# Attention at the layer border: 0.4 chunk for each q, and second-block steps between the last q

## The chip, the cores and the metric

The kernel runs on one core of a Trainium2 chip. TensorE (PE), VectorE (DVE), ScalarE (ACT), GpSimd (POOL) and SyncE (SP) are five engines, each with its own queue of instructions; they wait for one another by semaphores. DMA queues, fed mostly by SP and POOL here, move data between HBM and SBUF. The metric is the device time of one execution in microseconds (us); the time of a kernel is the median of its runs.

## The reference

Two layers of a graph transformer on 2708 tokens with 512 features, 8 heads, float32 throughout. The adjacency matrix is sparse (a token has a few neighbours, at most 22 here), so attention needs only the listed neighbours of each token. One layer, cut to what is computed:

```python
q = (h @ Wq.T + bq).reshape(n, N_HEADS, D_K)      # k and v likewise
scores = jnp.einsum('nhd,mhd->hnm', q, k) / jnp.sqrt(D_K)
scores = jnp.where(mask[None, :, :] == 0, -1e9, scores)   # mask = adj + eye
ctx = jnp.einsum('hnm,mhd->nhd', softmax(scores), v).reshape(n, D_MODEL)
h1 = layer_norm(h + ctx @ Wo.T + bo, ln1_g, ln1_b)
ff = relu(h1 @ W1.T + b1) @ W2.T + b2             # D_FF = 2048
h2 = layer_norm(h1 + ff, ln2_g, ln2_b)            # the next layer's h
```

Layer 0's h2 is layer 1's h.

## The kernel before

Tokens are sorted by their number of neighbours and cut into 22 tiles of 128 (the last has 20). Two tiles make a block, eleven blocks make a layer; the first block of a layer is tiles 21 (20 rows, 2 chunks of neighbours) and 20 (128 rows, 3 chunks), the second is tiles 19 (3 chunks) and 18 (4 chunks).

**Attention** is a generator, `attend`. A chunk is up to two neighbours of every token of a tile. For each chunk POOL gathers the rows of k and v by an indirect DMA (line 982) into one of five kv buffers; DVE multiplies k with q (L1019) and reduces per head to scores (L1025); a step later ACT takes the exponential (L1038) and, for the chunk's second neighbour, scales v head by head (L1045, eight small copies), DVE scales the first neighbour's v (L1051) and adds to the sum (L1058). After a tile's last chunk come its sums (L1066 to L1081) and the division on ACT (L1089), which leaves `cx`. Each `next` of the generator emits one such step and yields its cost: 1.0 for a chunk of two neighbours, 0.5 for one, 0.2 for an empty step. After the first block there are three empty steps, so its eight steps cost 1.0 + 0.5 + 1.0 + 1.0 + 0.5 + 3 x 0.2 = 4.6.

**Pacing.** `advance(more)` adds to a credit (at most 1.5) and emits steps while the credit is above zero and fewer than two finished tiles lie in `got`. `through(k)` emits steps until block k's tiles are in `got`, whatever the credit.

**The border** is the stretch between layer 0's last feed-forward and layer 1's first. There the projections of q of layer 1 run on PE: sixteen tiles, each four matmuls of 512 columns (L569), an evacuation on DVE (L1226) into one of three row buffers, and a write of q to HBM by SP (L1236). The first eight read transposed tokens that were loaded ahead (`pool`), the last eight are streamed: `queries` loads a tile's tokens by SP (L1213), yields, and projects it at the next call. Between the projections the loop advances the first block's attention. Then `through(0)` makes sure that the block is complete; `attended` transposes `cx` (L1128, evacuated as `cT` by ACT, L1133), loads the block's residual `xb` (L979, SP), multiplies by Wo (L569, `o`), adds and normalises (L1254, then L1112 to L1122, with a power on POOL, L1118). Behind that the last of the streamed steps run: two projections of q and the last write. Then `turned` transposes h (L1128) into `hT` (L1133, ACT), and the feed-forward (L1296, L1304, L1284) begins, with the second block's attention between its steps. A tile's q is read back by SP (L979) when its attention begins.

**Order.** The orders of PE, ACT and SP are those in which the program emits instructions. In the border DVE's is by hand as well, for what is emitted there; elsewhere a scheduler places DVE's and POOL's instructions, and it can place later DVE work of attention between those of the border.

The border in the code begins at line 1485 with:

```python
            with tc.manual_schedule(engines={mybir.EngineType.DVE}):
                for _ in range(2):
                    now.query(*pool.pop(0))
                next(ahead)
                next(streamed)
                while pool:
                    advance(0.5)
                    now.query(*pool.pop(0))
                for i in range(2 * AHEAD - 10):
                    advance(0.5)
                    next(streamed)
                through(0)
```

Of the kernel before, what the change touches and what calls it, by code (L numbers as in the profile page):

```python
# [471 lines left out]
def by_edges(ctx: ExitStack, tc: tile.TileContext, x, xT, adj, layers, out, good):  # L472
# [57 lines left out]
    def matrix(w, name, tag, by=None):  # L530
        src = chunked(w[name])
        t = wts.tile([P, src.shape[1], src.shape[2]], F32, tag=tag, name=tag)
        if by:
            by.dma_start(out=t, in_=src)
            return t
        k = max(1, src.shape[1] // 4)
        for c in range(0, src.shape[1], k):
            nc.sync.dma_start(out=t[:, c : c + k, :], in_=src[:, c : c + k, :])
        return t
# [32 lines left out]
    def finish(steps):  # L572
        for _ in steps:
            pass
# [416 lines left out]
    def asked(n, g):  # L991

        r = size(g)
        if g in own:
            return own.pop(g)
        if n == 0 and not all_made:
            return None
        q = at.tile([P, DM], F32, tag="q", name="q", bufs=QB)
        fetch(n, q, q_d[n], g)
        return q  # L1000
# [375 lines left out]
    def attend(n, got):  # L1376

        peak = small.tile([P, NT], F32, tag="peak", name="peak", bufs=1)
        nc.vector.memset(peak, 0.0)
        loaded = loads(n)  # L1380
        steps = []
        for g in order:
            cuts = chunks_of(g)
            steps += [(g, s0, c, i, i + 1 == len(cuts)) for i, (_, s0, c) in enumerate(cuts)]
            if g == order[1]:
                steps += [None] * 3
        steps += [None] * 3
        kv = next(loaded)
        yield 0.0
        q = asked(n, order[0])  # L1390
        done = [None] * 3
        for k, step in enumerate(steps):
            if step:
                g, s0, c, i, last = step
                if i == 0:
                    while q is None:
                        q = asked(n, g)
                        if q is None:
                            yield None
                    t, q = Tile(g, q), None  # L1400
                if k > 0:
                    kv = next(loaded)
                t.weights(kv, s0, c)
                if i > 0 and q is None and g != order[-1]:
                    q = asked(n, order[order.index(g) + 1])
                done.append((t, kv, s0, c, last))
            else:
                done.append(None)
            t3, t2, t1 = done[-4:-1]
            if t1:  # L1410
                t1[0].weigh(*t1[1:4])
            if t2 and t2[-1]:
                t2[0].sums(peak)
            if t3 and t3[-1]:
                got[t3[0].g] = t3[0].divided()
            yield c / SLOTS if step else 0.2
        nc.vector.tensor_reduce(flags[:, 4 + n : 5 + n], peak, AX.X, ALU.max)
        nc.vector.tensor_scalar(
            flags[:, 4 + n : 5 + n], flags[:, 4 + n : 5 + n], SAFE, None, ALU.is_le
        )  # L1420
# [3 lines left out]
    def advance(more):  # L1424

        nonlocal credit
        credit = min(credit + more, 1.5)
        while credit > 0 and len(got) < CXB - 1:
            cost = next(ahead, None)
            if cost is None:  # L1430
                break
            credit -= cost

    def through(k):

        while blocks[k][-1] not in got:
            next(ahead)
# [40 lines left out]
    for n in range(NL):  # L1478
        last = n == NL - 1
        nxt = None if last else Layer(n + 1, layers[n + 1])  # L1480
        if n > 0:
            streamed = now.queries(order[8 : 2 * AHEAD])
            got = {}
            ahead = attend(n, got)
# [3 lines that stand above are left out]
                next(ahead)  # L1488
                next(streamed)
                while pool:  # L1490
                    advance(0.5)
                    now.query(*pool.pop(0))
                for i in range(2 * AHEAD - 10):
                    advance(0.5)
                    next(streamed)
                through(0)
                early[n] = now.attended(blocks[0], got)
                next(early[n])
                for _ in blocks[0]:
                    next(early[n])  # L1500
                finish(streamed)
            now.load_w2(NFC // 2 - 1)
        *_, hs = early[n]
        hT = now.turned(blocks[0], hs)
        turning = projecting = None
        in_order = ExitStack()
        if n == 0:
            in_order.enter_context(tc.manual_schedule(engines={mybir.EngineType.Pool}))
        for k, block in enumerate(blocks):
            more = k + 1 < NB  # L1510
            asking = iter(())
            if n > 0 and k + AHEAD < NB:
                asking = now.queries(blocks[k + AHEAD])
            for f, zs in enumerate(now.feed_forward(block, hs, hT)):
                if f == NFC:
                    break
                if f in (5, 6, 7, 8) and behind:
                    next(behind)
                if more and f == 10 + (k + n == 0):
                    through(k + 1)  # L1520
                    projecting = now.attended(blocks[k + 1], got)
                    next(projecting)
                if more and f == 11 + (k + n == 0):
                    for hs_next in projecting:
                        advance(0.5 if k else 0.0)
                advance(PACE[n] if k else 1.1 if f < 11 else 0.4)
                if f in (0, 3, 7, 9):
                    next(asking, None)
                if more and f == NFC - 1:
                    finish(asking)  # L1530
                    hT = now.turned(blocks[k + 1], hs_next)
                if k == 0 and len(now.w1) < NFC // 2 and f % 2 == 0:
                    now.load_w1(len(now.w1), nc.scalar)
                    now.load_w2(len(now.w2), nc.scalar)
                if n > 0 and (k, f) == (0, 2):
                    now.load_second(1, temp)
                if not last:
                    if (k, f) == (0, 10):
                        now.load_next()
                        now.kv = [matrix(nxt.w, "Wk", "wk", nc.scalar)]  # L1540
                    if (k, f) == (0, 13):
                        now.kv.append(matrix(nxt.w, "Wv", "wv", nc.scalar))
                    if (k, f) == (3, 2):
                        now.wq = matrix(nxt.w, "Wq", "wq")
                    if f == 1 and k in (1, 3):
                        i, name, scale = (1, "bk", 1.0) if k == 1 else (0, "bq", DK**-0.5)
                        turning = turned_row(now.cols[i], name, scale)
                        rows_of = now if k == 1 else nxt
                        setattr(rows_of, name, next(turning))
                    if f == 3 and k in (1, 3):  # L1550
                        finish(turning)
                if not last and not more:
                    if f % 2:
                        nxt.load_w1(f // 2)
                        if f > 2:
                            nxt.load_w2(f // 2 - 1)
                    if f == 6:
                        nxt.load_first()
                        nxt.load_second(0, temp)
                    if f == 7:  # L1560
                        finish(ahead)
                        pool += nxt.preloaded(order[:8], temp)
            in_order.close()
            if not last:
                behind = now.keys_values(block, zs)
            if more:
                hs = hs_next
        finish(ahead)
        if last:
            checked()  # L1570
        else:
            nxt.wq = now.wq
            for _ in range(2):
                nxt.query(*pool.pop(0))
            nxt.kept()
            for g in order[:2]:
                own[g] = asked(n + 1, g)
            finish(behind)
            behind = None
            now = nxt  # L1580
# [63 lines left out]
```

## Time and profile before

| what | us |
|---|---|
| median of 3 runs | 1968.01 |
| lowest and highest run | 1963.77, 1973.71 |
| the profiled execution | 1964.63 |
| its span, first to last instruction | 1962.9 |
| PE busy in it | 1901.0 |
| DVE, ACT, POOL busy | 1300.8, 933.8, 796.8 |
| first q of layer 1 on PE to the first feed-forward matmul of layer 1 | 1138.33 to 1228.88 |

Times in the profile are microseconds from the span's start. A busy engine is one with an instruction in flight. A timeline row has start, duration, engine, line of the kernel, operation, tiles and shapes, number of instructions merged, and in brackets the idle time of the engine before it with what ended it. A PE matmul in float32 leaves two records, so x8 are four matmuls. A table of stretches gives busy times by engine, then the TensorE clock that was granted (1.00 is full) and the share of the DMA engines' time in use.

### The profile page before, as it was taken

The page shows a single profiled execution, that of the slowest core. Times are in us where ns is not written, and L with a number is a line of the kernel's source. Part 1 is how long each engine was busy: PE and PEld are TensorE (multiplying, and loading weights), DVE is VectorE, ACT ScalarE, POOL GpSimd, SP SyncE. Part 2 cuts the span into 40 slices and gives each one's busy share as a digit, 9 for nine tenths or more (in the row PEclk, how much of TensorE's full clock was granted, in tenths as well). Part 3 has the DMA queues.
Part 4 walks back from the last instruction along what each step waited for, and adds up shares of the span by engine and source line. Part 5 has one row for each costly group of instructions (what it writes and reads, how often), then busy time and mean ns, then how long its engine had stood idle before and what let it go on. Part 6 is the DMA issues. An engine that isn't in the chain of part 4 may idle for free. (4 is left out here: it accounts for less than half of the span.)

```text
span 1962.9 us, 20872 instructions
## 1 busy us (share of the span) xinstructions
PE 1901.0 (97%) x6162; PEld 1100.6 (56%) x6162; DVE 1300.8 (66%) x2142; ACT 933.8 (48%) x3219; POOL 796.8 (41%) x710
## 2 busy tenths in 40 slices
PE   8999988999999999999999998999999999999997
PEld 4444444565565655566556643556666566666664
DVE  5884587685867869659442036888688988877421
ACT  4660254564555655547332112756456765755410
POOL 3114635453555535425310022555347655644210
PEclk9999999999999999999999999999999999999998
DMA  9998766455655556546310646856455766554000
GB/s 327 352 311 307 258 211 235 161 166 189 202 161 199 188 186 227 161 150 204 130 43 27 230 162 215 298 174 217 153 177 198 247 214 209 186 190 154 34 11 13
DMA packets 131486, 366.92 MB, mean 187 GB/s; under 512 B 16668, under 2 KB 36988, under 8 KB 128654
## 3 DMA queue, kind: packets, MB, share of 16 engines
q0 software_dynamic: 69120, 246.35, 37.9%
q1 hardware_dynamic: 53332, 99.66, 14.9%
q10 hardware_dynamic: 8910, 19.48, 2.6%
q8 instruction: 50, 0.82, 0.2%
q14 instruction: 74, 0.61, 0.1%
HBM read 314.62 MB, written 50.83 MB: 186 GB/s over the span
## 5 line engine op out<-in xcount | busy, mean ns | idle before, releaser
L982 POOL DMA_INDIRECT kv<-kv_d,idx x420 | 546.1, 1300 | 475.9 <-DVE acc L1058 319.1
L1284 PE MATMUL a<-w,ft 128*128 128x512 f32 (+1 forms) x1408 | 669.9, 601 | 10.8 <-ACT ft L1304 9.5
L1296 PE MATMUL pf<-hT,w 128*128 128x256 f32 (+1 forms) x2816 | 636.3, 373 | 13.2 <-ACT ft L1304 8.8
L1296 PEld LDWEIGHTS pf<-hT,w 128*128 128x128 f32 x2816 | 521.1, 191 | 192.2 <-issue 107.3
L1284 PEld LDWEIGHTS a<-w,ft 128*128 128x128 f32 (+1 forms) x1408 | 256.5, 187 | 239.0 <-issue 201.4
L1304 ACT ACTIVATE ft<-pf,b 128x256 f32<-128x256 f32 (+1 forms) x352 | 158.5, 459 | 424.8 <-PE pf L1296 424.5
L1019 DVE TENSOR_TENSOR kv<-kv,q 128x1024 f32<-128x1024 f32 (+3 forms) x222 | 256.5, 1158 | 156.3 <-DMA kv<-kv_d,idx 103.7
L1045 ACT ACTIVATE kv<-kv,p 128x64 f32<-128x64 f32 x1232 | 311.0, 335 | 5.0
L1025 DVE TENSOR_REDUCE sc<-kv 128x16 f32<-128x1024 f32 (+3 forms) x222 | 255.2, 1154 | 1.4
L1058 DVE TENSOR_TENSOR acc<-acc,kv 128x1024 f32<-128x1024 f32 (+2 forms) x178 | 204.0, 1146 | 26.7 <-ACT kv L1045 25.9
L1118 POOL TENSOR_TENSOR rd<-va,mhalf 128x1 f32<-128x1 f32 (+1 forms) x88 | 85.4, 971 | 267.6 <-DVE va L1116 266.2
L1038 ACT ACTIVATE p<-sc,minus 128x8 f32<-128x8 f32 (+1 forms) x420 | 103.4, 295 | 161.1 <-DVE sc L1025 154.6
L569 PE MATMUL o<-wo,cT 128*128 128x512 f32 (+1 forms) x352 | 157.8, 601 | 3.7 <-DVE qs L1226 3.3
L1051 DVE TENSOR_TENSOR kv<-kv,p 128x512 f32<-128x512 f32 (+1 forms) x178 | 121.6, 684 | 52.8 <-ACT p L1038 52.7
L569 PEld LDWEIGHTS o<-wo,cT 128*128 128x128 f32 (+1 forms) x352 | 65.5, 187 | 92.2 <-issue 80.9
L1089 ACT ACTIVATE cx<-acc,su 128x64 f32<-128x64 f32 (+1 forms) x352 | 88.4, 333 | 42.6 <-DVE su L1081 33.9
L1316 DVE TENSOR_TENSOR h<-a,h 128x512 f32<-128x512 f32 (+1 forms) x44 | 29.7, 677 | 106.8 <-PE a L1284 106.7
L1122 DVE SCALAR_TENSOR_TENSOR h<-h,rd,ln_b 128x512 f32<-128x512 f32 (+1 forms) x88 | 65.9, 749 | 50.9 <-POOL rd L1118 50.9
L663 ACT ACTIVATE code<-aj 128x2708 bf16<-128x2708 int32 (+1 forms) x22 | 73.2, 3329 | 49.1 <-POOL aj L659 45.4
L1355 POOL DMA_INDIRECT kv_d<-kvs,ident_i x22 | 23.7, 1077 | 179.0 <-ACT kvs L1349 110.9
L666 DVE MAX8 tops<-code 128x8 f32<-128x247 f32 (+2 forms) x242 | 83.1, 400 | 19.3 <-ACT code L663 19.3
L1045 ACT ACTIVATE acc<-kv,p 128x64 f32<-128x64 f32 (+1 forms) x352 | 88.8, 334 | 1.4
(133 smaller groups left out, 1514.2 us busy)
## 6 DMA issues: line engine op xcount, KB each, us to landing
aj<-in_adj SPq DMA_DIRECT2D x21, 1354.0 KB, 8.0
kv_d<-kvs ACTq DMA_DIRECT2D x21, 512.0 KB, 5.6
w<-in_W SPq DMA_DIRECT2D x20, 512.0 KB, 4.8
xg<-in_xT SPq DMA_DIRECT2D x19, 512.0 KB, 8.8
kv<-kv_d,idx POOLq DMA_INDIRECT x420, 5.6
w<-in_W ACTq DMA_DIRECT2D x12, 512.0 KB, 8.9
q_d<-qs SPq DMA_DIRECT2D x22, 256.0 KB, 4.2
zT_d<-zT SPq DMA_DIRECT2D x22, 256.0 KB, 5.3
```

Of the source, the lines that this page charges most:

```text
L569: nc.tensor.matmul(o[:r], xs(c), wm[:, c, :], start=(c == 0), stop=(c == NC - 1))
L982: nc.gpsimd.indirect_dma_start(out=to, out_offset=None, in_=table[:, :], in_offset=bass.IndirectOffsetOnAxis(ap=s, axis=0), bounds_check=N ...
L1019: nc.vector.tensor_tensor(kv[:r, :c, :DM], kv[:r, :c, :DM], self.q[:r].unsqueeze(1).to_broadcast([r, c, DM]), ALU.mult,)
L1025: nc.vector.tensor_reduce(self.sc[:r, s0 : s0 + c, :], kv[:r, :c, :DM].rearrange("p s (h d) -> p s h d", d=DK), AX.X, ALU.add,)
L1038: nc.scalar.activation(p[:r, s, :], self.sc[:r, s, :], AF.Exp, bias=minus[:r, g, s : s + 1])
L1045: nc.scalar.activation(to[:, i, hd], kv[:r, i, DM + h * DK : DM + (h + 1) * DK], AF.Copy, scale=p[:r, s0 + i, h : h + 1],)
L1051: nc.vector.tensor_tensor(to[:, 0, :].rearrange("p (h d) -> p h d", d=DK), kv[:r, 0, DM:].rearrange("p (h d) -> p h d", d=DK), p[:r, s0, : ...
L1058: nc.vector.tensor_tensor(self.acc[:r, :c, :], self.acc[:r, :c, :], kv[:r, :c, DM:], ALU.add)
L1089: nc.scalar.activation(cx[:r, hd], self.acc[:r, 0, hd], AF.Copy, scale=self.su[:r, h : h + 1])
L1284: nc.tensor.matmul(a[:r], fts[f][:, c0 : c0 + r], self.w2[f // 2][:, f % 2, :], start=(f == 0), stop=(f == NFC - 1),)
L1296: nc.tensor.matmul(pf[:, :w], self.w1[f // 2][:, c, f % 2 * P : f % 2 * P + P], hT[:, c, :w], start=(c == 0), stop=(c == NC - 1),)
L1304: nc.scalar.activation(ft[:, :w], pf[:, :w], AF.Relu, bias=self.b1[:, f : f + 1])
```

## The change

Both loops of projections advance attention by 0.4 in place of 0.5 for each q. The last streamed steps, which ran straight through, now have an advance of 0.6 behind each of them; there are three such steps: a projection, a projection, and the last write.

```diff
@@ -1488,17 +1488,18 @@
                 next(ahead)
                 next(streamed)
                 while pool:
-                    advance(0.5)
+                    advance(0.4)
                     now.query(*pool.pop(0))
                 for i in range(2 * AHEAD - 10):
-                    advance(0.5)
+                    advance(0.4)
                     next(streamed)
                 through(0)
                 early[n] = now.attended(blocks[0], got)
                 next(early[n])
                 for _ in blocks[0]:
                     next(early[n])
-                finish(streamed)
+                for _ in streamed:
+                    advance(0.6)
             now.load_w2(NFC // 2 - 1)
         *_, hs = early[n]
         hT = now.turned(blocks[0], hs)
```

The advances behind the streamed steps emit steps of the second block, at a place where DVE's order is by hand.

## The prediction, made before the changed kernel ran

> **What bounds the kernel now.** I read the page's busy shares first, then a table of stretches across the border between the layers, then the timelines of TensorE (PE), VectorE (DVE) and ScalarE (ACT) there, and last the DMA issues of SyncE (SP).
>
> ```profile
> PE 1901.0 (97%) x6162; PEld 1100.6 (56%) x6162; DVE 1300.8 (66%) x2142; ACT 933.8 (48%) x3219; POOL 796.8 (41%) x710
> ```
>
> ```profile
> 1190.00:1200.00 10.00, 9.53 (x23) 3.98 (x22) 10.00 (x13) 1.47 (x6) 3.36 (x3) 1.00 0.68 212
> 1200.00:1205.00 5.00, 3.79 (x10) 1.53 (x9) 3.40 (x9) 2.02 (x8) 1.93 (x2) 1.00 0.91 304
> 1205.00:1210.00 5.00, 1.79 (x10) 0.77 (x9) 0.69 (x1) 0.78 (x4) 0.00 (x0) 0.87 0.86 315
> 1210.00:1217.00 7.00, 6.48 (x9) 1.26 (x10) 0.59 (x1) 0.59 (x3) 0.00 (x0) 0.60 0.31 89
> ```
>
> PE is busy for 97% of the span: a change wins only where PE idles or has a low clock. A row of the table is stretch and length, busy time of PE, weight loads, DVE, ACT and POOL, then granted clock, DMA share, GB/s. From 1205 to 1217 PE first idles and then works at clock 0.60. PE's timeline (start, duration, idle before it and its releaser) gives the reasons:
>
> ```profile
> 1180.91 7.03 PE L569 MATMUL q<-wq,zT 128*128 128x512 f32 x16
> 1189.67 3.70 PE L569 MATMUL q<-wq,zT 128*128 128x512 f32 x8 [1.74 <-DVE qs L1226]
> 1193.84 7.10 PE L569 MATMUL q<-wq,zT 128*128 128x512 f32 x16 [0.47 <-DMA zT<-zT_d]
> 1202.15 3.70 PE L569 MATMUL q<-wq,zT 128*128 128x512 f32 x8 [1.21 <-DVE qs L1226]
> ...
> 1210.07 6.30 PE L569 MATMUL o<-wo,cT 128*20 128x512 f32 x8 [3.27 <-DVE qs L1226]
> ...
> 1220.37 7.03 PE L569 MATMUL q<-wq,zT 128*128 128x512 f32 x16
> 1227.33 1.01 PE L1128 MATMUL tp<-ident,h 20*128 20x20 f32 x8
> 1228.88 4.31 PE L1296 MATMUL pf<-hT,w 128*128 128x148 f32 x32 [0.54 <-ACT hT L1133]
> ```
>
> Four stalls, 6.69 us, stand before the first o; from 1228.88, the start of the first feed-forward (FF), PE is busy without a gap until 1400. So 1228.88 is my yardstick: a shift there is carried to the end. DVE and ACT show whom PE waits for:
>
> ```profile
> 1187.74 1.23 DVE L1019 TENSOR_TENSOR kv<-kv,q 128x1024 f32<-128x1024 f32 x1 [3.09 <-DMA q<-q_d]
> 1188.99 1.22 DVE L1226 SCALAR_TENSOR_TENSOR qs<-q,bq 128x512 f32<-128x512 f32 x2
> ...
> 1209.23 0.69 DVE L1226 SCALAR_TENSOR_TENSOR qs<-q,bq 128x512 f32<-128x512 f32 x1 [5.83 <-DMA q_d<-qs]
> 1216.41 0.68 DVE L1254 TENSOR_TENSOR h<-o,xb 20x512 f32<-20x512 f32 x1 [6.49 <-PE o L569]
> ```
>
> ```profile
> 1216.41 1.14 ACT L1133 ACTIVATE cT<-tp,bv 128x128 f32<-128x128 f32 x4 [9.38 <-PE o L569]
> 1227.79 1.82 ACT L1133 ACTIVATE hT<-tp,b 128x20 f32<-128x20 f32 x8 [10.23 <-PE tp L1128]
> ```
>
> The kv line at 1187.74 is already the second block's (tile 19): DVE stalls there 3.09 us for that tile's q, with a finished q evacuation (L1226) queued behind it. The last evacuation waits 5.83 us, because its row buffer is still being written out. ACT is idle for 10.23 us before hT.
>
> ```profile
> DMA to landing us min/median/max: 3.2/4.4/7.5
> ```
>
> That is the 14 writes q_d<-qs from 1160 to 1230.
>
> [...]after 3.27 us idle one o took 6.30 us, where others of its shape take 3.43 (half of the x16 pitch), so 2.87 us lost. [...]
>
> **The change part by part.** The durations are of one profiled execution: span 1962.9, run 1964.63, which is 3.4 below the median 1968.01. I re-timed the border from the changed kernel's instruction order, built and not run, with each instruction at the duration of its row and each DMA at a landing time from this trace. Done so for the order of before, with 5.2 us for a write and 5.0 for a load, FF comes out at 1222.3, 6.6 early; the low clock (2.87), the slow q load (1.9) and the slow last write (1.8) are these 6.6. So those three are priced on their own below.
>
> *Loop at 0.4.* Ten advances give 4.0 instead of 5.0 of credit, but the first block's eight steps cost 4.6, and through(0) makes up the rest, so no work of the first block is removed. What changes is DVE's order: tile 19's three L1019/L1025 pairs (6 x 1.2 = 7.2 us) no longer stand between the q evacuations, and the 3.09 stall goes with them. The evacuation of 1188.99 can come at about 1184.7, the next when a q_d write issued at 1180.3 lands (4.4 later, 1184.7). PE's q then run on without a stall: two from 1180.91 to 1187.8, four more at 3.43 to 1201.5, 1.0 for the transposes, o at 1202.5 instead of 1210.07: 7.6 us earlier. It also comes warm (2.87). o for both tiles ends at 1202.5 + 6.9 + 0.6 (the cT wait, as now 0.46) = 1210.0 instead of 1220.37. **Gain here 10.4 us.** What is late next: not PE.
>
> *Advances behind the last three streamed steps.* They execute two steps of tile 19 before the FF: both weights, the first weigh, and by the order the second weigh too (on ACT before hT). Work is moved here from the first FF, where it was covered by PE. Now the path goes through DVE and ACT:
>
> - The order puts tile 18's first two L1019 into the norm of h: the first directly behind the 20-row L1254, with BNStats queued behind. It needs tile 18's q. On SP that load stands behind two xb loads and the last qs write. The 128-row xb load waits for a write issued at about 1199.0 to land (4.4 to 4.7: 1203.7), then two issues of 0.45: the q load goes out at 1204.6. To land takes 4.5 (median of q<-q_d) to 6.9 (1180.84 to 1187.74 in this border). I take 5.4: 1210.0. DVE, free at 1206.8, stalls 3.2 us.
> - From there both norms: before, L1254 to the next L1226 took 1216.41 to 1224.16 = 7.75. Without the first L1254 (0.69) and the 0.5 wait for o, plus two L1019 (2.3) of which 0.6 fills norm gaps: 8.3. L1226 at 1218.3.
> - Then 0.6 + 1.13 + 1.2 + 1.13 + 1.13 (a reduce of tile 18 that also got in) + 1.2 = 6.4: the second score at 1224.7.
> - ACT's two exps and eight copies of that chunk (0.48 + 2.02, less overlap: 2.4) stand in front of hT: hT starts at 1227.1. FF began 1.09 after hT before, so now at **1228.2: 0.7 earlier** than 1228.88. Of the gain of 10.4, 9.7 is eaten.
> - PE is done with its q at 1216.9 and has only transposes until 1228.2; it stalls about 9 us in front of FF, so FF starts at the low clock: +2.8 as in the measured case[...].
>
> Sum: -0.7 + 2.8 = **+2.1 us**. Tile 19's third weigh and ft are in time: ft is needed four pf (at least 4.4 us) after FF's start. POOL's four gathers for tile 18 wait for the first block's adds (L1058), which come earlier, so they go out some 3 to 6 us before 1195.68; rd (L1118), which both norms wait for, stands behind them in POOL's queue as before and is not held up. What is queued behind the new wait on DVE is BNStats, both norms and the last two q evacuations; PE's transposes of h, then hT and FF, wait for those.
>
> *Later.* DVE enters the first FF some 7 us further with the second block. PE had no gap there before, so this buys nothing until 1400. PE idles 9.8 us in all between 1400 and 1840 (the deficits of 40 us stretches); I put a change there at 0, bounds -3 to +3, since both credits fill the same gates (two tiles in got, cap 1.5).
>
> **The rivals.**
> - A, clear gain: the q of tile 18 and the scores come in time and hT waits for PE alone. FF would start at 1210.0 + 6.9 + 1.5 = 1218.4, 10.5 earlier and warm: 1957.5. For it: ACT idles 10.23 us there. Against: the two scores stand behind both norms in a strict queue. 5%.
> - B, slower: SP's chain is late. Writes at 7 and the q load at 6.9, as the worst here, put the stall's end at 1214.5, FF at 1232.7[...]: +7.2. If it ends after 1216.6, the loss passes 9.8 us (0.5%): about 1979. For it: 7.5 us landings at DMA share 0.9. Against: with the gathers earlier, the share at 1203 to 1210 should be lower. 17%.
> - C, nothing: all that is gained is eaten and the clock stays high, because q and transposes keep PE active: 0 to -1, 1967.5. 20%; it counts as no change.
>
> **How the numbers follow.** The forecast has 58%. Predicted: 1968.0 + 2.1 = 1970. From -0.4 (writes 4.0, loads 4.5[...]) to +7.2, with -3 to +3 of the later stalls and the spread of the runs before (-4.2 to +5.7): 1963 to 1979. 0.5% (9.8 us) is about what a measurement of this kernel can tell from no change. Faster 6%, same 76% (forecast, C, and rests of A and B), slower 18%.
>
> **What would show it.** Right: no L1226 stall of PE between 1187 and 1202, o at about 1202.5 in 3.6 us; DVE's L1019 in the norm waiting for q_d; hT on ACT behind 16 kv copies; PE idle 8 to 9 us before the first pf, with clock under 0.8 after it. Wrong: FF's start away from 1226 to 1233, PE stalls in the first FF, or later gaps changed by over 3 us.

## The result, and the profile after

| | before | after |
|---|---|---|
| median of 20 runs each | 1965.64 us | 1975.80 us |
| lowest and highest | 1961.04, 1973.71 | 1969.88, 1985.47 |
| ratio after to before, 95% interval | | 1.0049 (1.0036 to 1.0061) |
| the profiled execution, its span | 1964.63, 1962.9 | 1974.57, 1972.8 |

The ratio is 9.6 us (7.1 to 12.0): the change costs about as much as the 0.5% that the prediction called the edge of what can be told, and about 7.5 us more than it forecast. Single executions of one kernel differ by several us, and part of the 9.9 us between the two spans lies ahead of the border: the first q of layer 1 starts at 1138.33 before and at 1141.67 after, 3.3 us later, and up to there both kernels have the same instructions in the same order. So I count from that q. It leaves 6.6 us in this pair.

The page's busy shares, of after:

```profile
PE 1902.6 (96%) x6162; PEld 1102.8 (56%) x6162; DVE 1302.5 (66%) x2142; ACT 933.5 (47%) x3219; POOL 789.7 (40%) x710
```

The work is the same: PE is busy for 1.6 us longer, and the rest is idle time. The table of stretches across the border, of after (busy time of PE, weight loads, DVE, ACT, POOL; granted clock; DMA share; GB/s):

```profile
1200.00:1205.00 5.00, 5.00 (x13) 2.19 (x12) 0.69 (x1) 0.16 (x1) 0.00 (x0) 1.00 1.03 410
...
1217.00:1229.00 12.00, 5.36 (x19) 2.42 (x17) 11.42 (x16) 4.42 (x18) 1.54 (x2) 0.84 0.06 22
1229.00:1240.00 11.00, 9.44 (x39) 7.48 (x40) 6.51 (x9) 9.24 (x40) 3.55 (x3) 0.71 0.99 347
```

DVE has almost nothing to do from 1200 to 1205 (0.69 us), where it was busy for 3.40 of 5 us before, and the DMA engines' share is 1.03 there, 0.91 before. From 1217 to 1229 it is the other way: DVE is busy throughout, PE for 5.36 of 12 us, and PE then works at clock 0.71. PE's timeline of after:

```profile
1195.38 10.54 PE L569 MATMUL q<-wq,zT 128*128 128x512 f32 x24 [0.67 <-DMA zT<-zT_d]
...
1206.80 3.60 PE L569 MATMUL o<-wo,cT 128*20 128x512 f32 x8
...
1221.35 1.01 PE L1128 MATMUL tp<-ident,h 20*128 20x20 f32 x8
1230.56 6.63 PE L1296 MATMUL pf<-hT,w 128*128 128x148 f32 x32 [8.20 <-ACT hT L1133]
...
1263.98 1.27 PE L1296 MATMUL pf<-hT,w 128*128 128x148 f32 x8 [2.77 <-ACT ft L1304]
```

The stalls on L1226 are gone and o is warm: 3.60 us at a granted clock of 1.00, where before's took 6.30 at 0.56. Where no clock stands below, warm and cold go by the duration. Before the feed-forward (FF) PE waits 8.20 us for hT, and its first 32 matmul records take 6.63 us at clock 0.64, in place of 4.31 at 1.00. The last line is new: a stall of 2.77 us in the first FF, where before had none. DVE and ACT, of after, show whom PE waits for:

```profile
1211.99 1.22 DVE L1019 TENSOR_TENSOR kv<-kv,q 128x1024 f32<-128x1024 f32 x1 [0.87 <-DMA q<-q_d]
...
1238.87 1.22 DVE L1019 TENSOR_TENSOR kv<-kv,q 128x1024 f32<-128x1024 f32 x1 [4.49 <-DMA kv<-kv_d,idx]
```

```profile
1223.67 0.49 ACT L1038 ACTIVATE p<-sc,minus 128x8 f32<-128x8 f32 x2 [12.10 <-DVE sc L1025]
...
1227.06 0.49 ACT L1038 ACTIVATE p<-sc,minus 128x8 f32<-128x8 f32 x2 [0.85 <-DVE sc L1025]
1227.59 2.02 ACT L1045 ACTIVATE kv<-kv,p 128x64 f32<-128x64 f32 x8
1229.51 1.77 ACT L1133 ACTIVATE hT<-tp,b 128x20 f32<-128x20 f32 x8
...
1261.64 2.02 ACT L1089 ACTIVATE cx<-acc,su 128x64 f32<-128x64 f32 x8
1263.57 0.91 ACT L1304 ACTIVATE ft<-pf,b 128x148 f32<-128x148 f32 x3
```

PE's transposes of h begin at 1221.35, but hT is evacuated at 1229.51 only: two chunks of tile 19 (L1038, L1045) stand ahead of it in ACT's queue, and ACT idles 0.85 us for the second one's score, though the transposes that hT reads were done at 1222.36. I call such a chunk's work on ACT a weigh. At 1263.57 the same happens in the first FF: three ft come out in one go behind tile 18's cx, and PE waited for the first of them.

### The profile page after: what moved, and what is told of

It is laid out like the page before. It is cut to its first block, busy times and chain, and to the rows that moved or that the text cites. A ratio compares the mean times of both kernels' runs of the same rounds, so it can differ in the third digit from the quotient of the medians.

```text
span 1972.8 us, 20872 instructions
## 1 busy us (share of the span) xinstructions
PE 1902.6 (96%) x6162; PEld 1102.8 (56%) x6162; DVE 1302.5 (66%) x2142; ACT 933.5 (47%) x3219; POOL 789.7 (40%) x710
## 5 line engine op out<-in xcount | busy, mean ns | idle before, releaser
L982 POOL DMA_INDIRECT kv<-kv_d,idx x420 | 536.6, 1278 | 489.9 <-DVE acc L1058 333.7
L1045 ACT ACTIVATE kv<-kv,p 128x64 f32<-128x64 f32 x1232 | 311.0, 335 | 5.0
L1038 ACT ACTIVATE p<-sc,minus 128x8 f32<-128x8 f32 (+1 forms) x420 | 103.4, 295 | 177.8 <-DVE sc L1025 171.3
L1051 DVE TENSOR_TENSOR kv<-kv,p 128x512 f32<-128x512 f32 (+1 forms) x178 | 121.3, 682 | 49.4 <-ACT p L1038 49.4
L569 PEld LDWEIGHTS o<-wo,cT 128*128 128x128 f32 (+1 forms) x352 | 65.1, 186 | 86.5 <-issue 74.7
L1045 ACT ACTIVATE acc<-kv,p 128x64 f32<-128x64 f32 (+1 forms) x352 | 88.9, 335 | 1.4
```

Of the source, the lines that this page charges most:

```text
L569: nc.tensor.matmul(o[:r], xs(c), wm[:, c, :], start=(c == 0), stop=(c == NC - 1))
L982: nc.gpsimd.indirect_dma_start(out=to, out_offset=None, in_=table[:, :], in_offset=bass.IndirectOffsetOnAxis(ap=s, axis=0), bounds_check=N ...
L1038: nc.scalar.activation(p[:r, s, :], self.sc[:r, s, :], AF.Exp, bias=minus[:r, g, s : s + 1])
L1045: nc.scalar.activation(to[:, i, hd], kv[:r, i, DM + h * DK : DM + (h + 1) * DK], AF.Copy, scale=p[:r, s0 + i, h : h + 1],)
L1051: nc.vector.tensor_tensor(to[:, 0, :].rearrange("p (h d) -> p h d", d=DK), kv[:r, 0, DM:].rearrange("p (h d) -> p h d", d=DK), p[:r, s0, : ...
```

## The experiments

All kernels differ from before or after only in the border and in the first FF. The table, in us, counts in profiled executions from the first q of layer 1 on PE to the first FF matmul, and from there to the end of the span; "o" is the start of the first o, also from that q. "ft" is what PE then waits for ft in the first FF. A profiled execution isn't always a typical one: those of pace only, advances only and three scores were the fastest of their kernel's runs, those of hT first and rest in the FF the slowest.

| kernel | o | first q to FF | FF to end | pf x32 | ft | timed ratio to before (95%) |
|---|---|---|---|---|---|---|
| before | 71.7 | 90.6 | 734.0 | 4.31 | none | 1 |
| before, again | 71.2 | 90.3 | 733.7 | 4.32 | none | |
| after | 65.1 | 88.9 | 742.2 | 6.63 | 2.77 | 1.0049 (1.0036 to 1.0061) |
| after, again | 66.3 | 90.2 | 740.3 | 6.04 | 3.49 | 1.0051 (1.0036 to 1.0067) |
| pace only | 67.8 | 83.9 | 733.6 | 4.32 | none | 0.9984 (0.9974 to 0.9993) |
| advances only | 68.6 | 92.1 | 739.8 | 6.91 | 2.06 | 1.0043 (1.0027 to 1.0059) |
| hT first | 69.6 | 85.7 | 743.3 | | 5.45 | 1.0021 (1.0013 to 1.0028) |
| W2 early | 69.5 | 93.3 | 741.3 | 6.24 | 2.81 | 1.0067 (1.0051 to 1.0082) |
| no weigh | 66.0 | 82.1 | 739.5 | 4.31 | 3.40 | 1.0008 (1.0000 to 1.0016) |
| one weigh | 68.6 | 86.6 | 742.3 | 5.98 | 2.60 | 1.0038 (1.0023 to 1.0053) |
| two weighs | 69.6 | 90.0 | 741.2 | 6.11 | 3.88 | 1.0038 (1.0027 to 1.0049) |
| three scores in the gaps | 73.6 | 89.8 | 738.0 | 4.31 | 3.47 | 1.0037 (1.0025 to 1.0048) |
| two scores in the gaps | 73.0 | 89.2 | 741.8 | 4.32 | 5.18 | 1.0037 (1.0021 to 1.0053) |
| rest in the FF | 69.2 | 92.3 | 740.1 | 6.93 | none | 1.0040 (1.0025 to 1.0056) |

### The two halves of the change

The pace alone (after, without the advances):

```diff
-                for _ in streamed:
-                    advance(0.6)
+                finish(streamed)
```

> The loops at 0.4, but the last three streamed steps run straight through as before. Theory T (it is the advances behind the last q that take tile 19's steps out of the scheduler's hands and so out from between the q evacuations; the pace by itself moves little): tile 19's multiplies still stand between the q evacuations on DVE, PE keeps its stalls on L1226 there, first feed-forward within 2 us of that of before, total within 4 us of before (about 1965). Rival P, the prediction's own wording (the pace of 0.4 takes tile 19's work away): o warm and about 9 us earlier, first feed-forward near 1219, total 1956 to 1959.

The advances alone (after, with the old pace):

```diff
-                    advance(0.4)
+                    advance(0.5)
```

at both places.

> The loops at 0.5 as before, but an advance of 0.6 behind each of the last three streamed steps. Theory T: the whole change is in this part: o warm and 9 us earlier, hT behind two weighs, a stall of 7 to 9 us of PE in front of the first feed-forward, total within 4 us of after (1972 to 1979). Rival P (the advances only cost, the pace alone gains): PE's stalls on L1226 among the q stay, o as late as before, and the weighs come on top: first feed-forward 8 us or more later than before, total 1980 or more.

Measured: 1961.48 and 1972.69 us, against 1964.66. The loss is in the advances, and the pace of 0.4 alone is a small gain of 3.2 us (1.4 to 5.1): it beats both kernels. PE and DVE of the pace alone, a line of each timeline:

```profile
1220.84 4.32 PE L1296 MATMUL pf<-hT,w 128*128 128x148 f32 x32 [0.54 <-ACT hT L1133]
```

```profile
1186.04 1.22 DVE L1019 TENSOR_TENSOR kv<-kv,q 128x1024 f32<-128x1024 f32 x1 [2.92 <-DMA q<-q_d]
```

Tile 19's multiply still stands among the q evacuations and waits there for its q, 2.92 us as against 3.09 before: so T is right on what moves DVE's order, and the prediction's attribution of it to the pace falls. Yet T's start of FF within 2 us of before's was wrong: the last evacuation no longer waits for its row buffer (5.83 us before), PE has no stall ahead of o, o is warm (3.60 us), and FF starts 6.6 us sooner from the first q. Ahead of FF only DVE's order differs from before's, and little: one q evacuation now stands ahead of tile 19's third multiply and score, with a few attention steps changing places around it. DVE of the pace alone, and of before, where it is the first of the two:

```profile
1195.37 0.67 DVE L1226 SCALAR_TENSOR_TENSOR qs<-q,bq 128x512 f32<-128x512 f32 x1
```

```profile
1201.47 1.22 DVE L1226 SCALAR_TENSOR_TENSOR qs<-q,bq 128x512 f32<-128x512 f32 x2
```

That is 58.4 us after the first q in place of 63.1, and with three row buffers it is this one's buffer that the last evacuation takes over. So its write lands in time, though the scores stay where they were. That this move alone does it is argued, not tried apart. This profiled execution was the fastest of the kernel's 14, so 6.6 is not its typical gain; 3.2 is. From FF on it takes 733.6 us, where before takes 734.0: here a shift of FF's start is carried to the end. PE of the advances alone:

```profile
1192.46 12.23 PE L569 MATMUL q<-wq,zT 128*128 128x512 f32 x24 [2.43 <-DMA zT<-zT_d]
...
1229.11 6.91 PE L1296 MATMUL pf<-hT,w 128*128 128x148 f32 x32 [7.96 <-ACT hT L1133]
```

It has every feature of after: no stall on L1226, the long wait for hT, the slow pf, and the stall on ft that the table gives. T expected o 9 us earlier than before; from the first q it is 3.2 us earlier. The halves don't add up to the whole: -3.2 and +8.4 by the ratio are 5.2, against 9.6. In after the scores are gone from between the evacuations anyway, so the pace may have nothing left to gain there.

### hT ahead of the advances; W2 loaded early

```diff
-                for _ in streamed:
-                    advance(0.6)
+                finish(streamed)
+                *_, hs = early[n]
+                hT = now.turned(blocks[0], hs)
+                for _ in range(3):
+                    advance(0.6)
             now.load_w2(NFC // 2 - 1)
...
```

> As after, but h is turned (transposes and the eight hT evacuations on ACT) before the three advances of 0.6, which still stand where DVE's order is by hand. Theory T1 (after loses its gain because two weighs on ACT and the scores on DVE stand in front of hT): o warm and 9 us earlier, hT waits for PE's transposes alone, feed-forward 9 to 10 us earlier than in after (relative to the start of the border), warm, total 1956 to 1962. Rival T2 (the second block's attention is needed in time in the first feed-forward, so work taken out of the border comes back as stalls there): feed-forward starts early, but PE then waits for ft or cT in the first feed-forward for 6 us or more, total 1964 or more.

```diff
+                now.load_w2(NFC // 2 - 1)
                 for i in range(2 * AHEAD - 10):
...
-            now.load_w2(NFC // 2 - 1)
```

> As after, but the last 512 KB of W2 are loaded before the streamed q and not behind the border. Theory T3 (in after the gather of tile 18's third chunk lands late, since 512 KB of W2 and five other loads are issued just ahead of it, and DVE, whose order has that chunk's multiply ahead of tile 19's last adds, stalls 4.49 us, which PE pays with 2.77 us later): the stall on that gather under 2 us, no PE stall on ft near the eighth pf, total 2 to 4 us below after (about 1972). Rival R (the gather is late because its buffer comes free late, the traffic does not matter): stall over 3.5 us, total as after.

hT first: 1968.90 us, 5.5 us below after by the ratios (1.0021 and 1.0049), and the two intervals don't overlap; but it isn't the gain that T1 promised. Rival T2 is nearer: PE waits 5.45 us for ft, where 6 or more were expected. PE and ACT of it:

```profile
1227.68 3.31 PE L1296 MATMUL pf<-hT,w 128*128 128x148 f32 x24 [0.54 <-ACT hT L1133]
...
1235.61 2.34 PE L1296 MATMUL pf<-hT,w 128*128 128x148 f32 x8 [4.62 <-ACT ft L1304]
```

```profile
1233.27 2.02 ACT L1045 ACTIVATE kv<-kv,p 128x64 f32<-128x64 f32 x8
1235.19 0.36 ACT L1304 ACTIVATE ft<-pf,b 128x148 f32<-128x148 f32 x1
```

FF starts at once and warm, with 24 records in 3.31 us, but now the two weighs stand ahead of the first ft, and PE can run only three pf ahead of it. The stall has moved by one position in ACT's queue.

W2 early: 1978.99 us, above after if anything, so T3 falls. DVE of it:

```profile
1244.99 1.23 DVE L1019 TENSOR_TENSOR kv<-kv,q 128x1024 f32<-128x1024 f32 x1 [5.62 <-DMA kv<-kv_d,idx]
```

The gather is waited for even longer with the 512 KB out of its way. FF starts later from the first q than in any other kernel here. Rival R fits better: in both kernels POOL is idle for 8.52 us until DVE is past tile 19's first L1051, whose kv buffer is then free, and only then starts the chunk's two gathers, at 1228.38 in after and at 1233.36 here. POOL of after:

```profile
1228.38 1.89 POOL L982 DMA_INDIRECT kv<-kv_d,idx  x1 [8.52 <-DVE qs L1226]
```

### None, one and two weighs ahead of hT

Three kernels that differ only in what stands for the last streamed steps; the diff is of no weigh against after. DVE's order by hand is one stretch from the border through step 5 of the first FF, so that neither tile 19's scores nor tile 18's multiplies can move ahead of their place:

```diff
-            with tc.manual_schedule(engines={mybir.EngineType.DVE}):
+            hand.enter_context(tc.manual_schedule(engines={mybir.EngineType.DVE}))
...
-                for _ in streamed:
-                    advance(0.6)
+            finish(streamed)
...
+                if (k, f) == (0, 5):
+                    hand.close()
```

and with `for _ in streamed: advance(0.3)`, or `advance(0.6)`, in place of `finish(streamed)`.

> DVE's order by hand in one stretch from the border through step 5 of the first feed-forward, loops at 0.4, last streamed steps straight through: none of tile 19's work between the q evacuations, and no weigh on ACT in front of hT (the order there is hT, ft, weigh, ft, weigh). Theory T1 (each weigh in front of hT delays the feed-forward by its score on DVE and its copies on ACT, some 3 us, and nothing else takes the gain): hT waits for PE's transposes alone, feed-forward 8 to 10 us earlier than in after from the start of the border, total 1955 to 1961. Rival T2 (scores of tile 19 that are not done in the border are missing in the first feed-forward): PE stalls there on ft or on cT, 5 us or more in sum, total 1964 or more.

> The same with advances of 0.3 behind the streamed steps, which put two scores on DVE and one weigh on ACT in front of hT. T1: between the kernel with no weigh and that with two, about 3 us from each in the start of the feed-forward; total 1963 to 1969. Rival C (the low clock after PE's idle time is the whole cost, so that one weigh costs as much as two once PE has idled long enough): feed-forward starts as in the kernel with two weighs within 1 us, or pf is as slow.

> The same with advances of 0.6: two weighs in front of hT as in after, but tile 18's multiplies stay behind tile 19's on DVE and out of the norm of h. T1: about 3 us above the kernel with one weigh and 1 to 4 us below after, since two multiplies (2.4 us) leave the norm and no gather of tile 18 stands in front of tile 19's last adds; no PE stall on ft near the eighth pf; total 1968 to 1974. Rival N (tile 18's place in DVE's order doesn't matter): as after, 1973 to 1977.

Measured: 1966.35, 1971.12 and 1971.97 us against 1964.28. First q to FF is 82.1, 86.6 and 90.0 us. Of these steps 2.6 and 1.0 us lie ahead of o, where the three kernels have the same order on every engine and PE waits longer for zT (1.55, 2.48 and 3.58 us): that isn't the weighs'. From o to FF it is 16.1, 18.0 and 20.4 us. So the first weigh costs 1.9 us, and pf, behind 2.43 us of idle time of PE, takes 5.98 us in place of 4.31; the second costs 2.4 us more, and pf, behind 4.88 us, is hardly slower (6.11). T1, with 3 us for each, has the right kind and too large a size, and rival C is right that pf is as slow with one as with two. In after's two profiles o to FF takes 23.8 and 23.9 us. Up to hT its DVE differs from that of two weighs only by tile 18's two multiplies in the norm and one reduction of tile 18, so these, with the wait for q (0.87), cost the other 3.4.

But the times don't follow: T1 expected 1955 to 1961 for no weigh and 1963 to 1969 for one; only for two, with 1968 to 1974, does its total hold. With no weigh FF starts over 8 us sooner than in before's two profiles, and the kernel is still no faster than before. PE, and a table of stretches, of no weigh:

```profile
1222.20 4.31 PE L1296 MATMUL pf<-hT,w 128*128 128x148 f32 x32 [0.55 <-ACT hT L1133]
...
1256.96 1.27 PE L1296 MATMUL pf<-hT,w 128*128 128x148 f32 x8 [3.40 <-ACT ft L1304]
```

```profile
1221.00:1262.00 41.00, 36.91 (x153) 20.14 (x152) 38.63 (x47) 28.67 (x117) 20.03 (x15) 1.00 0.71 233
```

DVE is busy for 38.63 of 41 us. It has all of tile 19's scores still to do, and tile 18's cx ends later: the first FF is DVE's there, and PE pays. That is rival T2 in kind, though PE's waits for ft and cx there are 3.55 us, not 5. The scores that before does between the q evacuations are work done for the first FF. They needn't cost a stall: the pace alone keeps them, stalls for 2.84 us ahead of o in place of 6.69, and has no wait in the first FF.

With two weighs, no multiply of tile 18 stands in the norm, and DVE has no wait for a gather before 1258; yet PE, of that kernel, waits for ft longer than in after's two profiles (2.77 and 3.49):

```profile
1265.68 1.95 PE L1296 MATMUL pf<-hT,w 128*128 128x148 f32 x8 [3.88 <-ACT ft L1304]
```

So PE's stall comes without the wait of 4.49 us for a gather that is so plain in after's DVE. Gathers may still have a part in it: at 1258.52 DVE waits 2.92 us for one, ahead of tile 18's last score. Whether this order of DVE gains anything in time isn't settled: its interval and after's overlap.

### Second profiles of both kernels

> The changed kernel once more, for a second profile. Theory Z (the border's q run at what the loads of zT allow, and their landing differs from execution to execution): PE's idle time on zT among the q differs from the 0.67 us of the first profile, up to 3.3 us, with q after it at the low clock, and the final time differs by as much. Rival F (the profile of after is fixed): zT stall 0.5 to 1.0 us again, o warm at the same distance from the start of the border within 1 us.

> The kernel before once more, for a second profile. Theory W (the cold first o of the first profile, 6.30 us behind 3.27 us of idle time, is not in every execution, so that part of the gain that the prediction counted at the border does not exist in most): first o warm at about 3.6 us, first feed-forward 2 to 4 us earlier from the start of the border than in the first profile. Rival S (it is the same in each): o again above 6 us, feed-forward within 1 us of the first profile, counted from the start of the border.

PE of after, again, and of before, again:

```profile
1196.27 10.54 PE L569 MATMUL q<-wq,zT 128*128 128x512 f32 x24 [1.88 <-DMA zT<-zT_d]
...
1265.14 1.64 PE L1296 MATMUL pf<-hT,w 128*128 128x148 f32 x8 [3.49 <-ACT ft L1304]
```

```profile
1210.58 6.53 PE L569 MATMUL o<-wo,cT 128*20 128x512 f32 x8 [2.51 <-DVE qs L1226]
```

Theory W falls: before's o is cold in both executions (6.30 and 6.53 us), so that the gain the prediction saw there is real. Theory Z holds in part: the wait for zT is 1.88 in place of 0.67 and o comes 1.2 us later, but the q behind it stay warm (10.54 us) and this execution isn't the longer one (1973.72 and 1974.57). Six other kernels have the same order of DVE up to o. No weigh has o at 66.0 us; the other five (hT first, one weigh, two weighs, rest in the FF, and W2 early, which has that load in addition) have it 3.5 to 4.5 us later than after's first profile, with waits for zT (W2 early: for the evacuation) of 2.5 to 3.6 us and the q behind them at 12 us in place of 10.54. So o's place differs by up to 4.5 us between executions and kernels with the same order, and both profiles of after are at the short end. From the first q on they take 6.6 and 6.0 us more than before's first profile, less than the timed 9.6. Their whole executions, though, differ from before's two by 8.6 to 9.9 us: the rest lies ahead of the first q, which starts at 1141.67 and 1141.35 in after and at 1138.33 and 1139.36 in before.

### Tile 19's scores in DVE's gaps

From the kernel with no weigh; the first block's pace is 0.7, and:

```diff
             for i in range(2 * AHEAD - 10):
-                advance(0.7)
+                if i < 3:
+                    advance(0.7)
+                if i == 3:
+                    through(0)
                 next(streamed)
-            through(0)
+                if 3 <= i < 6:
+                    next(ahead)
```

(`i < 5` for two scores.)

> DVE by hand in one stretch as in the kernel with no weigh in front of hT, the first block finished sooner (0.7 for each q), and tile 19's three scores put by hand behind the last three q evacuations ahead of o, where DVE idled 2.7 us each; the two weighs that come with them stand on ACT ahead of cT, where ACT idled 7 us. Theory T2 (the second block's attention has to be under way when the first feed-forward starts, and DVE's and ACT's idle time among the q is the place for it): first feed-forward as early as with no weigh in front of hT (8 us earlier than before, from the border's start), PE's stall on ft in it under 1 us, total 1957 to 1962. Rival Q (scores among the q hold up the q evacuations, o or cT wherever they stand): o 2 us or more later than with no weigh, or cT waiting for ACT, total 1963 or more.

> The same with two scores among the last q and one weigh ahead of cT; the third score follows in the first feed-forward. T2: stall on ft between that of the kernel with none (3.40) and that with three, total 1958 to 1964. Rival Q: q evacuations held up as with three but less, total 1963 or more.

Measured: 1974.65 and 1972.64 us against 1965.71. T2's remedy falls, rival Q holds: o comes 7.7 and 7.1 us later than with no weigh. PE of three scores:

```profile
1196.56 13.00 PE L569 MATMUL q<-wq,zT 128*128 128x512 f32 x24 [3.92 <-DMA zT<-zT_d]
...
1212.04 3.61 PE L569 MATMUL o<-wo,cT 128*20 128x512 f32 x8 [1.54 <-ACT cT L1133]
...
1250.81 1.27 PE L1296 MATMUL pf<-hT,w 128*128 128x148 f32 x8 [3.26 <-ACT ft L1304]
```

zT is waited for longer, o waits for cT behind the weighs, and, though the second block is done sooner, an ft is late again. That stall now comes 23 us after FF's start, with three steps emitted ahead; in after, with two, it comes 33 us after the start, of which 2.3 are the slow pf.

### The place of cx in ACT's queue

The last theory comes from a comparison of ACT in before and after. Before:

```profile
1259.55 2.01 ACT L1089 ACTIVATE cx<-acc,su 128x64 f32<-128x64 f32 x8
1261.46 0.90 ACT L1304 ACTIVATE ft<-pf,b 128x148 f32<-128x148 f32 x3
```

Tile 18's cx starts 30.7 us after FF's start in before and 31.1 us in after: the block isn't finished sooner. But ahead of the block's end stand three ft behind cx in before and five in after, since two steps of attention were emitted in the border. PE needs the ft behind cx two steps sooner. The test lets attention rest for two steps:

```diff
-                advance(PACE[n] if k else 1.1 if f < 11 else 0.4)
+                if not (n > 0 and k == 0 and f in (3, 5)):
+                    advance(PACE[n] if k else 1.1 if f < 11 else 0.4)
```

> As after up to the third step of the first feed-forward; then no advance at its steps 3 and 5, so that tile 18's division (cx on ACT) stands three ft ahead of the block's end, as in the kernel before, and not five. Theory E (the stall in the first feed-forward is one of place in ACT's queue: the second block is finished 31 us after the feed-forward's start in before and after alike, but after emits it two steps sooner, so the ft behind it is one that PE needs two steps, about 7 us, sooner): last cx again 31 to 35 us after the start, PE's stall on the ft behind it under 1 us, hT and the start as in after, total 2 to 5 us below after (1969 to 1972). Rival G (the rate of DVE and of the gathers decides, and later emission makes the block later by as much): cx 37 us or more after the start, the stall 2.5 us or more again, total as after or above.

PE and ACT of it:

```profile
1233.99 6.93 PE L1296 MATMUL pf<-hT,w 128*128 128x148 f32 x32 [7.54 <-ACT hT L1133]
```

```profile
1264.39 2.02 ACT L1089 ACTIVATE cx<-acc,su 128x64 f32<-128x64 f32 x8
1266.32 0.63 ACT L1304 ACTIVATE ft<-pf,b 128x148 f32<-128x148 f32 x2
```

cx starts 30.4 us after FF's start, as before, and PE has no stall at all in the first FF: theory E is right on the stall. The time is another matter: 1973.50 us against 1965.25, where 1969 to 1972 was expected. Its interval overlaps after's. In its profile, of the slowest of its six runs, FF starts 2.0 to 3.4 us later from the first q than in after's two (its wait for zT is 2.91), and 1.6 and 1.4 us come back at 1309 and before 1392. FF to end is 740.1 us, hardly below after's 742.2 and 740.3, so what the stall's end is worth in time stays open.

## Why the prediction was right or wrong

The measured median lies in the range, and the mechanism at the border is the forecast one. The size is not: +2.1 us was forecast and +9.6 measured, and the largest missing part is in the step *Later*. That the median lies in the range is owed to the range's width, not to the sum. Times of the two kernels are compared from the first q, which takes 3.3 us off after's times in the first profile and 3.0 in the second.

1. **Removed stalls, o earlier and warm: right, a little too good.** o at 1202.5 was predicted; measured is 1206.80 less 3.3, so 1203.5, and 2.2 us behind the prediction in the second profile. It is warm, 3.60 us in both. The gain up to the end of both o was 9.3 instead of 10.4 (the next q at 1214.39 in place of 1220.37, and 3.3). What was late next was zT, which the prediction passed over with "What is late next: not PE": the DMA share rose to 1.02.
2. **Its cause was named wrongly.** "Loop at 0.4 ... What changes is DVE's order" belongs to the other half. The pace alone leaves tile 19's multiply where it was; the advances, standing in the stretch whose order is by hand, pin it behind the last q. Nor did the last evacuation's wait hang on that work: the pace alone ends it with the scores in place.
3. **DVE's wait for tile 18's q: 3.2 predicted, 0.87 and 1.00 measured.** The wait is shorter because DVE came to it 1.0 and 2.2 us later, at o's end. What counts for FF is where it ends: 1210.0 predicted, 1208.7 and 1210.0 measured. With it rival B (1214.5) is refuted; that its +7.2 is nearer to the measured total is luck. B's own sum is slightly off, too: 1199.0 with a write of 7, two issues of 0.45 and a load of 6.9 ends at 1213.8, and from its +7.2 at 1214.5 the loss passes 9.8 us when the stall ends at 1217.1, not 1216.6.
4. **hT behind two weighs: right.** hT at 1227.1 predicted, 1229.51 less 3.3 measured; FF at 1228.2 predicted, 1227.2 and 1228.6 measured. Experiments show what makes up the 23.8 us from o to FF: 16.1 with no weigh, 1.9 for the first weigh, 2.4 for the second, and 3.4 for tile 18's multiplies and reduction.
5. **Low clock: +2.8 predicted, +2.3 and +1.7 measured** (6.63 and 6.04 in place of 4.31). Behind 8.20 us of idle time the granted clock over these records was 0.64 in the first profile; before's o, behind 3.27 us, had 0.56, and the size was taken from it. The parts for the clock in B's +7.2 and in the range's -0.4 were the author's estimates, which no trace of before showed. Up to here the sum is +0.7 and +1.4 us: the border itself comes out below the +2.1 of the forecast.
6. **The failed step: "PE had no gap there before, so this buys nothing until 1400", with later stalls at 0, bounds -3 to +3.** The first FF lost 3.0 us in the first profile (the stall of 2.77) and 5.4 in the second (3.49, and the matmuls behind it, with a granted clock of 0.87 from 1262 to 1275: the pf took 1.64 in place of 1.17, the a behind it 3.33 in place of 2.09). What followed added 2.9 in the one and took 0.8 back in the other. The sums are 5.9 and 4.6 where 0 stood, outside the bounds. A PE stall in the first FF was one of the signs that the prediction had named for being wrong. The prediction followed tile 19's third weigh and found its ft in time; it should have followed tile 18's cx, the last thing of the block that stands ahead of an ft. Work emitted two steps sooner wasn't finished sooner (cx 31.1 us after FF's start, 30.7 before), and later ft waited for it in the order of ACT's queue: three come out at 1263.57, behind cx. Rest in the FF shows that this place makes the stall. It doesn't show that the place makes the loss: without the stall that kernel still takes 6.1 us more than before from FF to end, 2.6 of them the slow pf. What holds it up afterwards stays open.
7. **Rival A (FF at 1218.4) shows what the ideal was worth.** With no weigh FF starts 8.4 us sooner from the first q than before, and the kernel gains nothing, for DVE then has 7.2 us of scores more to do in the first FF. It was the scores between the evacuations that the first FF lived on, not the stalls: the pace alone keeps the scores, starts FF 6.6 us sooner in its profile, and keeps that to the end.

What remains: the timed 9.6 us against 6.6 and 6.0 in the profiles from the first q on. In these profiles the rest, 2.0 to 3.3 us, lies ahead of the first q, where the instructions are the same. Over the fourteen profiles that q starts between 1136.9 and 1142.2, at 1137.0 with the advances alone; whether after's late start is chance or has to do with the change isn't known. The spread of o (65 to 70 us after the first q in kernels with after's order of DVE up to there) is another possible place.

## What to carry to other kernels

Work pushed earlier in a program doesn't only cost where it lands: in a queue that runs in order, as ACT's did here ahead of hT, it takes a place ahead of what comes later, and if its inputs come no sooner, everything behind it waits, so follow the last result of the moved chain and see what is queued behind that. Before counting a removed stall as gain, ask whether work for the next stage goes with it: with the scores gone, a border 8 us shorter gained nothing; with the scores in place, the stall's end was a gain. Count from the point where the orders of two kernels part: the waits ahead of it, here for zT, differ between executions and needn't be the change's. Try the two halves of a change apart: here one was worth -3.2 us and the other cost 8.

## What the runs showed of the hardware

- **The low clock came behind idle time of PE, but not behind every wait of the same length.** A group of q behind 2.43 us of idle time took 12.23 us (advances alone, with a granted clock of 0.91 from 1185 to 1205), and behind 2.48 us 12.24 (one weigh), where behind 1.88 and 0.67 us it took 10.54 (at clock 1.00 behind the 0.67); an o behind 2.51 us took 6.53 in place of 3.60. Length alone doesn't settle it: a pf behind 2.60 us (one weigh) took 2.34 us, and one behind 3.40 us (no weigh, granted clock 1.00 from 1221 to 1262) 1.27, where others take 1.17. What else decides it wasn't shown.
- **DMA at a share of 1.02 to 1.03 moved 388 and 410 GB/s** from 1190 to 1200 and from 1200 to 1205 of after. What PE then waits for among the q is zT and no longer an evacuation: 0.67 and 1.88 us in after, 1.55 to 3.58 in five kernels with the same order of DVE up to there. So stalls of DVE that are taken away gave less than their length.
